# Macaron block of MoE and Mamba on one core: the scan's sum over states by accumulating transfers in SBUF, in two sums, in place of adds on GpSimd

## The chip, the core and the metric

The kernel runs on one core of a Trainium2 chip. A core has five engines with a queue of instructions each: TensorE (PE in the profile, with the weight loads as PEld), VectorE (DVE), ScalarE (ACT), GpSimd (POOL) and SyncE (SP, which here only issues DMAs). They meet through semaphores. SBUF and PSUM are the on-chip memories; transfers are made by 16 DMA engines. The metric is the time of one execution on the device in microseconds (us), the median of a few runs; less is better.

## What is computed

x has 4 sequences of 1024 positions with 128 features. Three sublayers follow each other, each on a layer norm of x: a dense mixture of 8 experts (added at half weight), a Mamba layer, and the same mixture once more. Cut to what matters:

```python
x = x + 0.5 * ffn(layernorm(x))      # sum over 8 experts of cw_e * (silu(x Wg_e) * (x Wu_e)) Wd_e
x = x + mamba(layernorm(x))
x = x + 0.5 * ffn(layernorm(x))

# mamba, 256 channels d, 16 states n
xs, z = split(x @ W_in)
xc = silu(conv4(xs) + conv_b)
dt, B, C = softplus(...), ..., ...   # projections of xc
h[t] = exp(dt[t] * A) * h[t-1] + dt[t] * xc[t] * B[t]     # for each d and n
y[t] = sum over n of h[t] * C[t] + D * xc[t]
out = (y * silu(z)) @ W_out
```

All of it is float32. The sum over n of h C is what the change is about.

## The kernel before, in words

The positions are cut into 8 blocks of 512 (two per sequence); a Mamba block holds its 256 channels as tiles of 128 partitions x 2 x 512, "128x1024" in the profile. There are 16 FFN stages (8 blocks, first and second FFN) in a fixed order (`order`), and TensorE's work on them paces everything: a stage has 16 halves of an expert each taking gate products into PSUM (pg, L543 to L545), up products (pu) and down products (pd, L612, or L598 and L606 where they are split). For each half, ScalarE takes silu of pg (L534) and DVE multiplies it with pu (L559); the next half's pu can't start before that. ScalarE copies pd out (L634); GpSimd (DVE in the first nine experts and in the last stage) weighs it with the broadcast gate weights cwb (L643) and adds it to acc (L646), which TensorE transposes at the end of a stage (L675).

Mamba work is laid between the FFN work by slots. A half has four slots; `run_events` runs at each slot and releases the events of all chains that are due (`START`, `WIDE`, `LATE` and the like give due slots; an event with a condition may wait up to 12 slots longer). A small planner (`Plan`) keeps a model of the time at which each engine will be free. DVE's work is put into two lists, `hi` and `lo`, with a cost and a time from which it is ready; `fill` issues what is due before TensorE's present time. All engines' queues get exactly the order in which Python issues the instructions, so an engine that waits holds back all that is behind it.

A block's states go in pairs (`two`, when `turn` allows it: the list `lo` has at most 9 entries). For each state n:

- ScalarE computes da = exp(dt A) (L861) into a tile of the pool "big" (11 buffers of 128x1024, which also holds dt, dx, cv, zs and the split halves hh, hl and weights wds);
- DVE, `prod` (L875): hb = dx * B into PSUM; B and C of the state are in bcb, which SP broadcasts from DRAM (L696, three buffers, the next one is asked for by `pump` when a product with C is issued);
- DVE, `step` (L887): two scans, one for each 128 channels. At the first it decides `aside` (L882 to L886): if GpSimd's planned backlog is below LOAD = 3.0 us and DVE's list `lo` holds more than LEFT = 6.0 us, the scan writes to da in SBUF and GpSimd makes the product with C; else it stays in PSUM;
- `read`: the last column is kept for the next block (L914 or L900); then da = h * C on DVE (L915), or on GpSimd for a state put aside (L903); then GpSimd adds da to y (L918 or L909). y starts as D * xc (ScalarE, L853).

GpSimd's instructions wait in the list `pend`, first in, first out. `pool_run`, called at each L875, issues from it against a credit of 5.8 us (CAP), and makes each instruction that it issues wait for that L875 (the reason given in the code is "shared SBUF port"). `pool_need` issues all up to a given entry when its result is needed.

When all states of a block are added (`scanned`), `gate` multiplies with silu(z) (GpSimd L944, or DVE L939 in blocks 0 and 7), `outproj` (L955) and `upd` (L962) add the result to x, and the second FFN of that block may begin with its norm statistics (L329 to L341) and gate weights (L418 to L469).

SP's queue holds, in order of issue, the loads of B and C (L696), the broadcasts of the gate weights (L499, L474), the blocks of x (`load_x`, L237; the event at L1048) and the stores of the result.

Of the kernel before, what the change touches and what calls it, by code (L numbers as in the profile page):

```python
# [45 lines left out]
NEVER = 1e9  # L46
WAIT = 12
LOAD = 3.0
LEFT = 6.0
QUEUE = 9  # L50

# [120 lines left out]
def tile_macaron_mamba_moe(  # L172
# [528 lines left out]
    riders, slot, burst_at, want = [], [0], [-1], set()  # L701
    pend, credit = [], [0.0]

    def pool_put(fn, cost, ready, first=False):
        it = [fn, cost, ready, False, None, first]
        pend.insert(sum(o[5] for o in pend) if first else len(pend), it)
        if not plan.lo:
            pool_run(None)
        return it

    def pool_run(after):
        credit[0] = min(credit[0] + CAP, CAP)
        while pend and (after is None or credit[0] > 0.0):
            pool_one(after)

    def pool_one(after):
        it = pend.pop(0)
        credit[0] -= it[1]
        ins = it[0]()
        it[3], it[4] = True, plan.on_pool(it[1], max(it[2], plan.dve))  # L720
        if after is not None:
            tc.add_manual_dep(
                ins.ins, after.ins.name, mybir.DependencyInfo(mybir.DependencyClass.Sync, mybir.DependencyReason.DATA),
                reason="shared SBUF port",
            )

    def pool_need(it):
        if it not in pend:
            plan.need(lambda: it[3])
        while not it[3]:  # L730
            pool_one(None)
        return it[4]


    def mamba_events(k):
# [111 lines left out]

        def dtfin():
            dx = d["dx"] = big(f"dx_{nm}")
            d["dx_it"] = plan.put(lambda: V.tensor_tensor(dx, d["dt"], d["xc"], ALU.mult), 1.14, d["spt"]) if fast else pool_put(lambda: G.tensor_tensor(dx, d["dt"], d["xc"], ALU.mult), 2.4, d["spt"])  # L850
            y = d["y"] = sb.tile([P, ND, TB], F32, tag="y", bufs=2, name=f"y_{nm}")
            d["y_it"] = [
                plan.act_put(lambda i=i: S.activation(y[:, i, :], d["xc"][:, i, :], AF.Copy, scale=D_sb[:, i : i + 1]), 0.61, 0.0)  # L853
                for i in range(ND)
            ]
# [22 lines left out]
        def step(n, i):  # L878
# [10 lines left out]
                0.0 if first else st_sb[:, i, n : n + 1], ALU.mult, ALU.add,  # L889
            )  # L890

        def read(n):
            hb = d.pop("hb")
            da = d.pop(("da", n))
            bcb = d.pop(("bcb", n))
            d.pop(("read", n))
            plan.act_need(*d["y_it"])
            if d["aside"]:
                if not last:
                    V.tensor_reduce(st_sb[:, :, n : n + 1], da[:, :, TB - 1 : TB], AX.X, ALU.max)  # L900

                def weigh():
                    ins = G.tensor_tensor(da, da, bcb[:, 1:2, :].to_broadcast([P, ND, TB]), ALU.mult)  # L903
                    ahead["free"] += 1
                    pump()
                    return ins

                pool_put(weigh, 2.4, plan.dve)
                it = pool_put(lambda: G.tensor_tensor(d["y"], d["y"], da, ALU.add), 2.4, plan.dve)  # L909
                if n == NS - 1:  # L910
                    d["scanned"] = it
                return
            if not last:
                V.tensor_copy(st_sb[:, :, n : n + 1], hb[:, :, TB - 1 : TB])  # L914
            V.tensor_tensor(da, hb, bcb[:, 1:2, :].to_broadcast([P, ND, TB]), ALU.mult)  # L915
            ahead["free"] += 1
            pump()
            it = pool_put(lambda: G.tensor_tensor(d["y"], d["y"], da, ALU.add), 2.4, plan.dve)  # L918
            if n == NS - 1:
                d["scanned"] = it  # L920

        def zproj(i):
                if i == 0:
# [8 lines left out]
        def gate():  # L932
            assert d["zp"] == ND
            d["yg"] = d.pop("zs")
            plan.need(lambda: "scanned" in d)

            if quick:
                def mul():
                    V.tensor_tensor(d["yg"], d["yg"], d["y"], ALU.mult)  # L939

                at = pool_need(d["scanned"])
                d["gated"] = plan.put(mul, 1.14, at)
                return
            d["gated"] = pool_put(lambda: G.tensor_tensor(d["yg"], d["yg"], d["y"], ALU.mult), 2.4, plan.dve)  # L944

        def outproj():
            if quick:
# [82 lines left out]
    def run_events(t):  # L1030
        slot[0] = t
        plan.fill(plan.pe)
        for ch in chains:
            while ch and ch[0][0] <= t:
                at, wait, f = ch[0][:3]
                if len(ch[0]) > 3 and t - at < wait and ch[0][3]() > plan.pe + 0.15:
                    break
                ch.pop(0)
                f()
        chains[:] = [ch for ch in chains if ch]  # L1040

    GPS = E
    add(0, [(0, lambda: load_expert(0))])
    for s in range(len(order)):
        add(8 * GPS * s, ffn_events(s))
        kind, k = order[s]
        if kind == 1 and k + 1 < NBLK:
            add(8 * GPS * s, [(2, lambda k=k: load_x(k + 1))])  # L1048
        add(8 * GPS * (s + 1), [(FENDS.get(s, 16), lambda s=s: ffn_end(s), lambda s=s: max(plan.bank_free(), summed(s)))])
    for k in range(NBLK):  # L1050
        front, mid, back = mamba_events(k)
# [65 lines left out]
```

## Time and profile before

| what | value |
|---|---|
| runs shown, us | 1286.93, 1288.33, 1288.80 (median 1288.33) |
| profiled execution: its own time / its span, us | 1286.3 / 1284.5 |
| ScalarE busy in the span | 70% |
| DMA: bytes moved, mean rate | 113.51 MB, 88 GB/s |
| SP's queue, share of the 16 DMA engines' time | 31.6% |
| GpSimd waiting for DVE's L875 before L918 | 49.0 us in 20 waits |
| starts of FFN stages 4 and 15 (TensorE's first pg) | 327.6 and 1206.3 us |
| updates of x by blocks 0 and 7 (L962) | 278.8 and 1159.1 us |

How to read the lines in the next part: the engine line gives busy time, share of the span and number of instructions. A line by groups has source line, engine, operation, output<-inputs, shapes and number; then busy time and mean nanoseconds of one; then the idle time of the engine just before them and who ended it. A line of waits has the waiting engine and line, whom it waited for, then total us, number of waits, the longest. A line of the chain of waits has start, duration and what was going on; one of the timeline has start, duration, engine, line, operation, and in brackets an idle time before it and its releaser. A line of a stretch gives busy time of PE, PEld, DVE, ACT and POOL, TensorE's granted clock, the share of the DMA engines and the rate.

### The profile page before, as it was taken

The page shows a single profiled execution, that of the slowest core. Times are in us where ns is not written, and L with a number is a line of the kernel's source. Part 1 is how long each engine was busy: PE and PEld are TensorE (multiplying, and loading weights), DVE is VectorE, ACT ScalarE, POOL GpSimd, SP SyncE. Part 2 cuts the span into 40 slices and gives each one's busy share as a digit, 9 for nine tenths or more (in the row PEclk, how much of TensorE's full clock was granted, in tenths as well). Part 3 has the DMA queues.
Part 4 walks back from the last instruction along what each step waited for, and adds up shares of the span by engine and source line. Part 5 has one row for each costly group of instructions (what it writes and reads, how often), then busy time and mean ns, then how long its engine had stood idle before and what let it go on. Part 6 is the DMA issues. An engine that isn't in the chain of part 4 may idle for free.

```text
span 1284.5 us, 14134 instructions
## 1 busy us (share of the span) xinstructions
PE 1255.9 (98%) x4728; PEld 852.4 (66%) x4728; DVE 1102.8 (86%) x1287; ACT 902.0 (70%) x1171; POOL 791.5 (62%) x590
## 2 busy tenths in 40 slices
PE   7999999999999999999999989999999999999998
PEld 5776666666666666666666656666666666668885
DVE  5875589998998999999988979997799999977675
ACT  5775777776778778775867768676877777646663
POOL 1012376767779767786786677787688668663400
PEclk9999999999999999999999999999999999999999
DMA  4420242433232433234333343332234333411110
GB/s 126 139 61 25 77 120 91 107 102 83 82 103 81 126 93 94 86 91 126 94 104 91 71 124 98 101 105 81 67 92 104 110 94 97 114 42 42 34 34 24
DMA packets 72201, 113.51 MB, mean 88 GB/s; under 512 B 7360, under 2 KB 20544, under 8 KB 72128
## 3 DMA queue, kind: packets, MB, share of 16 engines
q1 hardware_dynamic: 72128, 112.61, 31.6%
q8 instruction: 37, 0.61, 0.2%
q14 instruction: 36, 0.29, 0.1%
HBM read 109.71 MB, written 2.88 MB: 88 GB/s over the span
## 4 chain that ended last, share of the span: by engine, by line
PE 77%; DVE 7%; POOL 3%; issue 3%; ACT 3%; DMA 1%; SPq 0%; DVEq 0%; POOLq 0%; ACTq 0%
PE pd L612 23%; PE pu L543 8%; PE pu L544 7%; PE pu L545 7%; PE pg L543 7%; PE pg L545 7%; PE pg L544 7%; PE pd L598 2%; DVE h L559 2%; DVE hb_m L875 2%; DVE hb_m L887 1%; PE pd L606 1%; PE xs_m L767 1%; PE po_m L955 1%; PE dbl_m L813 1%
## 5 line engine op out<-in xcount | busy, mean ns | idle before, releaser
L559 DVE TENSOR_TENSOR h<-h,pu 128x1024 f32<-128x1024 f32 x256 | 311.2, 1216 | 128.8 <-PE pu L545 88.1
L612 PE MATMUL pd<-h,wd 128*128 128x512 f32 x848 | 404.5, 594 | 1.4 <-ACT acc L634 0.7
L534 ACT ACTIVATE h<-pg 128x1024 f32<-128x1024 f32 x256 | 262.8, 1026 | 163.0 <-PE pg L545 156.3
L543 PE MATMUL pg<-xh_f,wh 128*128 128x512 f32 x512 | 272.6, 532 | 1.3 <-ACT xh_f L384 0.7
L918 POOL TENSOR_TENSOR y_m<-y_m,da_m 128x1024 f32<-128x1024 f32 x95 | 229.0, 2410 | 50.0 <-DVE hb_m L875 49.0
L643 POOL TENSOR_TENSOR tmp<-tmp,cwb 128x512 f32<-128x512 f32 x98 | 130.0, 1327 | 182.3 <-ACT tmp L634 77.2
L612 PEld LDWEIGHTS pd<-h,wd 128*128 128x128 f32 x848 | 158.4, 189 | 116.9 <-issue 96.7
L543 PE MATMUL pu<-xh_f,wh 128*128 128x512 f32 x512 | 211.3, 413 | 4.8 <-DVE h L559 4.5
L545 PE MATMUL pg<-xh_f,wl 128*128 128x512 f32 x512 | 202.7, 396 | 0.0
L544 PE MATMUL pg<-xl_f,wh 128*128 128x512 f32 x512 | 202.3, 395 | 0.0
L544 PE MATMUL pu<-xl_f,wh 128*128 128x512 f32 x512 | 202.1, 395 | 0.0
L545 PE MATMUL pu<-xh_f,wl 128*128 128x512 f32 x512 | 202.0, 395 | 0.0
L875 DVE TENSOR_TENSOR hb_m<-dx_m,bcb_m 128x1024 f32<-128x1024 f32 x128 | 181.6, 1418 | 3.0 <-POOL dx_m L850 1.3
L861 ACT ACTIVATE da_m<-dt_m,A_sb 128x512 f32<-128x512 f32 x256 | 163.9, 711 | 0.6
L543 PEld LDWEIGHTS pg<-xh_f,wh 128*128 128x128 f32 x512 | 96.7, 189 | 67.1 <-issue 31.8
L646 POOL TENSOR_TENSOR acc<-acc,tmp 128x512 f32<-128x512 f32 x98 | 130.7, 1333 | 11.5 <-DVE hb_m L875 4.2
L544 PEld LDWEIGHTS pg<-xl_f,wh 128*128 128x128 f32 x512 | 97.1, 190 | 52.5 <-issue 38.9
L887 DVE TENSOR_TENSOR_SCAN hb_m<-da_m,hb_m 128x512 f32<-128x512 f32 x98 | 119.9, 1224 | 2.0
L543 PEld LDWEIGHTS pu<-xh_f,wh 128*128 128x128 f32 x512 | 96.4, 188 | 36.0 <-DVE h L559 11.6
L887 DVE TENSOR_TENSOR_SCAN hb_m<-da_m,st_sb,hb_m 128x512 f32<-128x512 f32 x92 | 118.1, 1284 | 2.1
L915 DVE TENSOR_TENSOR da_m<-hb_m,bcb_m 128x1024 f32<-128x1024 f32 x95 | 115.7, 1218 | 1.3
L544 PEld LDWEIGHTS pu<-xl_f,wh 128*128 128x128 f32 x512 | 96.4, 188 | 24.1 <-issue 3.6
(137 smaller groups left out, 1651.8 us busy)
## 6 DMA issues: line engine op xcount, KB each, us to landing
bcb_m<-bc_m SPq DMA_DIRECT2D x128, 512.0 KB
cwb<-cd_f SPq DMA_DIRECT2D x128, 256.0 KB
x<-in_L_attn_x_dram SPq DMA_DIRECT2D x8, 256.0 KB
wraw<-in_L_ffn_w_gate_dram SPq DMA_DIRECT2D x8, 256.0 KB
wraw<-in_L_ffn_w_up_dram SPq DMA_DIRECT2D x8, 256.0 KB
wd<-in_L_ffn_w_down_dram SPq DMA_DIRECT2D x8, 256.0 KB
out_dram<-x SPq DMA_DIRECT2D x8, 256.0 KB
cd_f<-ct_f SPq DMA_DIRECT2D x64, 4.0 KB
```

The source lines that it names most:

```text
L534: S.activation(h, pg, AF.Silu)
L543: T.matmul(o[:, q, :], wh[e][:, i, cols], d["xh"], start=True, stop=False)
L544: T.matmul(o[:, q, :], wh[e][:, i, cols], d["xl"], start=False, stop=False)
L545: T.matmul(o[:, q, :], wl[e][:, i, cols], d["xh"], start=False, stop=True)
L559: V.tensor_tensor(h, h, pu, ALU.mult)
L612: T.matmul(d["pd"], wd[e][:, cols], h[0], start=(f == 0), stop=(f == FC - 1))
L643: it = put(lambda: G_.tensor_tensor(t, t, cwb, ALU.mult), 1.25, at)
L646: it = put(lambda: G_.tensor_tensor(acc, acc, t, ALU.add), 1.25, at)
L861: S.activation(da[:, i, :], d["dt"][:, i, :], AF.Exp, scale=A_sb[:, i, n : n + 1])
L875: mul = V.tensor_tensor(hb, d["dx"], bcb[:, 0:1, :].to_broadcast([P, ND, TB]), ALU.mult)
L887: V.tensor_tensor_scan((da if d["aside"] else hb)[:, i, :], da[:, i, :], hb[:, i, :], 0.0 if first else st_sb[:, i, n : n + 1], ALU.mult, ...
L918: it = pool_put(lambda: G.tensor_tensor(d["y"], d["y"], da, ALU.add), 2.4, plan.dve)
```

## The change

The adds of da to y on GpSimd (L909 and L918) go. Each is replaced by a DMA that GpSimd issues with accumulate-add: da is added into y in SBUF by the transfer itself (`gather`). There are two sums per block. Even states add into y; state 1's own buffer da becomes the odd sum, into which the other odd states add; after the last state one more transfer adds the odd sum to y (`join`), and that is `scanned` now.

`pend` is no longer first in, first out: each entry belongs to a chain (the even and the odd sum of a block, dx, the FFN's weighted sums), order holds within a chain, and of the chains' heads the one that can start first is issued. A transfer can start when its product is planned to be ready and the transfer before it in its sum has landed, which is planned for 5.9 us after the issue (YDMA); its issue is planned at 0.9 us of GpSimd. Transfers aren't made to wait for an L875 and don't use up the credit. `pool_run` stops at a transfer that could not start within 1.5 us (AHEAD); `pool_flush` in `run_events` issues those that can start.

The rule for putting a state aside is not changed, but the backlog that it looks at has 0.9 us for a transfer where it had 2.4 for an add. `load_x` moves from 2 slots after to 12 slots before the start of a stage, except in the first.

```diff
@@ -46,6 +46,8 @@
 NEVER = 1e9
 WAIT = 12
 LOAD = 3.0
+YDMA = 5.9
+AHEAD = 1.5
 LEFT = 6.0
 QUEUE = 9
 
@@ -701,34 +703,63 @@
     riders, slot, burst_at, want = [], [0], [-1], set()
     pend, credit = [], [0.0]
 
-    def pool_put(fn, cost, ready, first=False):
-        it = [fn, cost, ready, False, None, first]
-        pend.insert(sum(o[5] for o in pend) if first else len(pend), it)
+    def pool_put(fn, cost, ready, chain="w", dma=None):
+        it = [fn, cost, ready, False, None, chain, dma]
+        pend.append(it)
         if not plan.lo:
             pool_run(None)
         return it
 
+    def pool_start(it):
+        at = max(it[2], plan.pool)
+        if it[6] is not None:
+            at = max(at, it[6].get("landed", 0.0))
+        return at
+
+    def pool_next():
+        heads, seen = [], set()
+        for it in pend:
+            if it[5] not in seen:
+                seen.add(it[5])
+                heads.append(it)
+        return min(heads, key=pool_start) if heads else None
+
     def pool_run(after):
         credit[0] = min(credit[0] + CAP, CAP)
         while pend and (after is None or credit[0] > 0.0):
-            pool_one(after)
-
-    def pool_one(after):
-        it = pend.pop(0)
+            it = pool_next()
+            if after is not None and it[6] is not None and pool_start(it) > max(plan.pool, plan.dve) + AHEAD:
+                break
+            pool_one(after, it)
+
+    def pool_one(after, it):
+        pend.remove(it)
+        ins = it[0]()
+        it[3] = True
+        if it[6] is not None:
+            plan.pool = pool_start(it) + it[1]
+            it[4] = it[6]["landed"] = plan.pool - it[1] + YDMA
+            return
         credit[0] -= it[1]
-        ins = it[0]()
-        it[3], it[4] = True, plan.on_pool(it[1], max(it[2], plan.dve))
+        it[4] = plan.on_pool(it[1], max(it[2], plan.dve))
         if after is not None:
             tc.add_manual_dep(
                 ins.ins, after.ins.name, mybir.DependencyInfo(mybir.DependencyClass.Sync, mybir.DependencyReason.DATA),
                 reason="shared SBUF port",
             )
 
+    def pool_flush():
+        while pend:
+            it = pool_next()
+            if it[6] is None or pool_start(it) > max(plan.pool, plan.pe - 1.0):
+                return
+            pool_one(None, it)
+
     def pool_need(it):
         if it not in pend:
             plan.need(lambda: it[3])
         while not it[3]:
-            pool_one(None)
+            pool_one(None, next(o for o in pend if o[5] == it[5]))
         return it[4]
 
 
@@ -847,7 +878,7 @@
 
         def dtfin():
             dx = d["dx"] = big(f"dx_{nm}")
-            d["dx_it"] = plan.put(lambda: V.tensor_tensor(dx, d["dt"], d["xc"], ALU.mult), 1.14, d["spt"]) if fast else pool_put(lambda: G.tensor_tensor(dx, d["dt"], d["xc"], ALU.mult), 2.4, d["spt"])
+            d["dx_it"] = plan.put(lambda: V.tensor_tensor(dx, d["dt"], d["xc"], ALU.mult), 1.14, d["spt"]) if fast else pool_put(lambda: G.tensor_tensor(dx, d["dt"], d["xc"], ALU.mult), 2.4, d["spt"], "x")
             y = d["y"] = sb.tile([P, ND, TB], F32, tag="y", bufs=2, name=f"y_{nm}")
             d["y_it"] = [
                 plan.act_put(lambda i=i: S.activation(y[:, i, :], d["xc"][:, i, :], AF.Copy, scale=D_sb[:, i : i + 1]), 0.61, 0.0)
@@ -889,6 +920,26 @@
                 0.0 if first else st_sb[:, i, n : n + 1], ALU.mult, ALU.add,
             )
 
+        lane = [{}, {}]
+
+        def gather(n, da, at):
+            q = n % 2
+            if n == 1:
+                d["odd"] = da
+            else:
+                to = d["odd"] if q else d["y"]
+                it = pool_put(lambda: G.dma_start(out=to, in_=da, accum_op=ALU.add), 0.9, at, (k, q), lane[q])
+            if n < NS - 1:
+                return
+
+            def join():
+                while any(o[5] == (k, 1) for o in pend):
+                    pool_one(None, next(o for o in pend if o[5] == (k, 1)))
+                return G.dma_start(out=d["y"], in_=d.pop("odd"), accum_op=ALU.add)
+
+            ready = max(at, lane[1].get("landed", 0.0)) + YDMA
+            d["scanned"] = pool_put(join, 0.9, ready, (k, 0), lane[0])
+
         def read(n):
             hb = d.pop("hb")
             da = d.pop(("da", n))
@@ -905,19 +956,15 @@
                     pump()
                     return ins
 
-                pool_put(weigh, 2.4, plan.dve)
-                it = pool_put(lambda: G.tensor_tensor(d["y"], d["y"], da, ALU.add), 2.4, plan.dve)
-                if n == NS - 1:
-                    d["scanned"] = it
+                pool_put(weigh, 2.4, plan.dve, (k, n % 2))
+                gather(n, da, plan.dve + 2.5)
                 return
             if not last:
                 V.tensor_copy(st_sb[:, :, n : n + 1], hb[:, :, TB - 1 : TB])
             V.tensor_tensor(da, hb, bcb[:, 1:2, :].to_broadcast([P, ND, TB]), ALU.mult)
             ahead["free"] += 1
             pump()
-            it = pool_put(lambda: G.tensor_tensor(d["y"], d["y"], da, ALU.add), 2.4, plan.dve)
-            if n == NS - 1:
-                d["scanned"] = it
+            gather(n, da, plan.dve + 0.1)
 
         def zproj(i):
                 if i == 0:
@@ -938,10 +985,10 @@
                 def mul():
                     V.tensor_tensor(d["yg"], d["yg"], d["y"], ALU.mult)
 
-                at = pool_need(d["scanned"])
-                d["gated"] = plan.put(mul, 1.14, at)
+                d["gated"] = plan.put(mul, 1.14, pool_need(d["scanned"]))
                 return
-            d["gated"] = pool_put(lambda: G.tensor_tensor(d["yg"], d["yg"], d["y"], ALU.mult), 2.4, plan.dve)
+            at = pool_need(d["scanned"])
+            d["gated"] = pool_put(lambda: G.tensor_tensor(d["yg"], d["yg"], d["y"], ALU.mult), 2.4, at, (k, 0))
 
         def outproj():
             if quick:
@@ -1030,6 +1077,7 @@
     def run_events(t):
         slot[0] = t
         plan.fill(plan.pe)
+        pool_flush()
         for ch in chains:
             while ch and ch[0][0] <= t:
                 at, wait, f = ch[0][:3]
@@ -1045,7 +1093,7 @@
         add(8 * GPS * s, ffn_events(s))
         kind, k = order[s]
         if kind == 1 and k + 1 < NBLK:
-            add(8 * GPS * s, [(2, lambda k=k: load_x(k + 1))])
+            add(8 * GPS * s, [(2 if s == 0 else -12, lambda k=k: load_x(k + 1))])
         add(8 * GPS * (s + 1), [(FENDS.get(s, 16), lambda s=s: ffn_end(s), lambda s=s: max(plan.bank_free(), summed(s)))])
     for k in range(NBLK):
         front, mid, back = mamba_events(k)
```

## Prediction

> **What bounds the kernel now.** I read the summary of engines first, then the busy time in the stretch where the change acts, then who waits for whom at TensorE, then the costliest groups. From the page:
>
> ```profile
> span 1284.5 us, 14134 instructions
> ...
> PE 1255.9 (98%) x4728; PEld 852.4 (66%) x4728; DVE 1102.8 (86%) x1287; ACT 902.0 (70%) x1171; POOL 791.5 (62%) x590
> ...
> PEclk9999999999999999999999999999999999999999
> ```
>
> TensorE is busy for 98% of the span at an undisturbed clock, and the diff changes no matmul. The time can fall only by what TensorE loses in waits. The state work (first product of states to last block's end) lies between about 100 and 1160 us; busy time there:
>
> ```profile
> core 0: us, PE busy (x) PEld busy (x) DVE busy (x) ACT busy (x) POOL busy (x), PEclk, DMA share, GB/s
> 100.00:1160.00 1060.00, 1049.00 (x3856) 691.89 (x3855) 945.39 (x1077) 761.38 (x992) 758.29 (x539) 1.00 0.34 93
> ```
>
> TensorE idles 1060.0 - 1049.0 = 11.0 us of this stretch, DVE is busy 89%, GpSimd 72%, the DMA engines 34%. "Idle" misses some waits: matmuls are pipelined (0.39 us long, started 0.23 us apart), so I also went through the start times of all matmuls in the trace and added up what each gap has beyond the usual gap between the same pair of lines: 41 us in all, some 24 of them between 100 and 1160 us. That 24 us (1.9%) is all that any relief of DVE or GpSimd can win. Who ends the waits of the weight loads, from the list of waits at TensorE:
>
> ```profile
> PEld pg L543 <- ACT h L534: 14.9, 31, 1.3
> PEld pu L543 <- DVE h L559: 11.6, 19, 1.9
> ...
> PEld v_m L834 <- DVE dbs_m L822: 5.9, 4, 3.7
> ...
> PEld cwt_f L467 <- POOL cw_f L458: 2.7, 5, 0.8
> ```
>
> (A weight load may wait 0.2 us at no cost, so these are more than matmuls lose: in the count by gaps, ScalarE's h is 6.5 us, DVE's h 6.2, DVE's dbs 4.9, GpSimd together some 2.) The largest single stall is one of dbs, and it isn't DVE's load that makes it. In the chain of waits and the timeline of DVE and TensorE:
>
> ```profile
> 732.94 3.35 POOL da_m L903
> ...
> 736.71 5.55 DMA x<-in_L_attn_x_dram
> 742.26 0.02 issue
> ```
>
> ```profile
> 742.28 0.87 DVE L329 BATCH_NORM_STATS2 st_f<-x 128x6 f32<-128x128 f32 x4 [3.44 <-DMA x<-in_L_attn_x_dram]
> ```
>
> ```profile
> 745.38 0.51 PE L834 MATMUL v_m<-dbs_m,wdt_h 128*128 128x512 f32 x1 [3.24 <-DVE dbs_m L822]
> ```
>
> SP's load of x stood behind two loads of B and C (L696) which waited for a buffer that GpSimd's C product (L903) held; the load landed 5.55 us after its issue, DVE's statistics stood still for 3.44 us with dbs queued behind them, and TensorE lost 3.4 us there and 0.9 us just after: 4.3 us.
>
> **The change, part by part.** The groups that it touches:
>
> ```profile
> L918 POOL TENSOR_TENSOR y_m<-y_m,da_m 128x1024 f32<-128x1024 f32 x95 | 229.0, 2410 | 50.0 <-DVE hb_m L875 49.0
> ...
> L875 DVE TENSOR_TENSOR hb_m<-dx_m,bcb_m 128x1024 f32<-128x1024 f32 x128 | 181.6, 1418 | 3.0 <-POOL dx_m L850 1.3
> ...
> L915 DVE TENSOR_TENSOR da_m<-hb_m,bcb_m 128x1024 f32<-128x1024 f32 x95 | 115.7, 1218 | 1.3
> ```
>
> ```profile
> L909 POOL TENSOR_TENSOR y_m<-y_m,da_m 128x1024 f32<-128x1024 f32 x33 | 83.4, 2527 | 2.5
> L903 POOL TENSOR_TENSOR da_m<-da_m,bcb_m 128x1024 f32<-128x1024 f32 x33 | 81.0, 2453 | 18.7 <-DVE hb_m L875 18.7
> ```
>
> 1. *Removed:* 95 + 33 = 128 adds on GpSimd, 229.0 + 83.4 = 312 us of its 791.
>
> 2. *Added:* per block 15 transfers (state 1 gives its own buffer to the odd sum) and one join, 8 x 16 = 128 transfers of 128x1024 f32, 512 KB each, issued by GpSimd. No such operation is in this trace. GpSimd's time for one issue: at least the 0.36 us that SP takes for a B and C load of the same size; at most a whole add, 2.4 us. I take the planner's 0.9, between the two and nearer to SP's row: 128 x 0.9 = 115 us, so GpSimd is relieved by about 200 us (bounds +5 and +266). Landing: the nearest row is the B and C load, 4.79 us on the chain of waits at 254.59 us; an add must also read its destination, so at most twice that, 9.6. I take 5.9, the planner's, nearer to the row. The Trainium skill, in "DMA: Bandwidth & Descriptors", section "Anatomy of one DMA", gives 2.0 us plus the bytes at 436 GB/s for a DMA issued by GpSimd, an estimate of 3.2 us; no run here shows it, and with 3.2 in place of 5.9 the forecast would not move.
>
> What waits for a landing: the next add of the same sum. 128 states take from 148 to 1136 us (first and last L875), 7.7 us each, so with two sums the next add comes 15.4 us later on average and some 10 us in a burst: 5.9 is covered, 9.6 just. Behind a transfer that does wait stand GpSimd's other instructions: norm statistics (L338 to L341), gate weights (L446 to L458), weighted sums (L643, L646).
>
> DMA engines: a B and C load is 256 packets of about 0.118 us on 16 engines, 1.9 us of them all; an add takes between that and twice that, so 128 of them 243 to 486 us, 23 to 46 points on 34%. B and C loads then land up to some 4 us later, hidden by three buffers: one is asked for when the product with C is done and needed two states, 15 us, later.
>
> One rule speaks against issuing from GpSimd. The copies that DVE makes of SBUF data are L914's, 49 in the whole trace, 7.7 us in all, 157 ns each. By "SBUF — State Buffer" of the Trainium skill, section "SBUF: two separate sides", GpSimd can't write descriptors while DVE runs such a copy in a two-port mode. No run here shows this; by it 7.7 us of GpSimd's time at most would be lost off TensorE's path, against none.
>
> 3. *More C products on GpSimd.* A state goes aside (L882 to L886) when GpSimd's backlog is under 3 us and DVE's list is over 6 us. Per state of 7.7 us GpSimd now has 2.4 (add) + 2.1 (weighted sums) + 0.6 (33 of 128 C products) + 0.4 = 5.5 us. With 0.9 for the add, the same load is reached when 0.87 of the states are aside; 0.26 are now. The list of over 6 us will often be missing when DVE is relieved; I take the middle, 0.55, that is 70 states: DVE loses 37 x 1.22 = 45 us (bounds 0 and 78 x 1.22 = 95), from 945 to 900 of 1060, 85%. DVE's L875 has a median of 1.23 us and a mean of 1.42: 128 x 0.19 = 24 us spent behind GpSimd's instructions; with 128 fewer adds and 37 more products perhaps a third goes, 8 us. All of this lies beside TensorE. What it is worth is a part of DVE's waits in the stretch: h 6.2 and the remaining dbs, xl and others some 4, together 10. With DVE down by 5 to 6% of its load I take a third: -3 us (bounds: 0 and -10; that the new order makes TensorE wait more is rival (b)).
>
> 4. *load_x* moves 14 slots (some 16 us) ahead of its place in SP's queue, for all stages but the first. x has six buffers and the old contents are stored a stage before, so it waits for none. It goes ahead of the B and C load that held it at 732 us: -4.3 us (bounds 0, if another SP wait takes its place, and -4.3). What is late next there is the wait for the buffers themselves, which DVE isn't behind.
>
> 5. *The end of a block.* The last add lands (5.9), the join lands (5.9), against one add of 2.4: the sum is ready some 10 us later. Cover: block 0's x is updated at 278.8 us and its second FFN starts at 327.6; block 7's at 1159.1, with the FFN at 1206.3. The preparations take some 16 to 20 us of these 47 to 49; without this cover it would be 10 us each, 20 in all.
>
> 6. *Buffers:* counted from the trace, at most 8 of the 11 "big" buffers hold live data. The odd sum keeps one for a whole block, and a second one where blocks meet: 10. ScalarE's exponentials would wait at 12.
>
> Sum, against the profiled execution (span 1284.5, its own time 1286.3): -4.3 - 3 = -7.3, about 1 us given back for transfers that GpSimd waits for: -6, so 1280. The median of the runs shown, 1288.33, is 2 above that execution, so **1282**, 0.5% below.
>
> **The rivals.** (a) *Only x counts*: DVE's load isn't what makes the short stalls (their releasers are the order of instructions, with 6.5 us on ScalarE), or few more states go aside: 1288.3 - 4.3 = 1284, down to no gain at all if x's stall reappears, 1288. For it: DVE's h waits are 19 waits of 0.6 us, scattered. (b) *Slower, waits at the head of GpSimd's queue*: a landing of over 10 us, the pace of a burst, makes the transfer hold back what TensorE needs: 16 gate weights, 16 sums, 24 norm statistics, 56 places. At 0.3 us lost at each, 17 us, less 4.3: +13, 1301; it decides from landings over 10 us, or from an issue that costs GpSimd as much as an add. For it: the DMA engines go to 57 to 80%, and no accumulating transfer has a row here. Against it: the 15.4 us mean spacing. (c) *Much faster*: all 10 us of DVE's waits, GpSimd's 2 and x go: 1288.3 - 16 = 1272. Against it: ScalarE's waits stay, and the fixed order is only a plan.
>
> **How the numbers follow.** Forecast (1277 to 1285): 0.48. (c): 0.07. (a): 0.14, half of it faster by over 0.2%, half within; 0.2% (2.6 us) is about what a measurement of this kernel can tell from no change. (b): 0.31, of which 0.02 within 0.2%. Faster 0.48 + 0.07 + 0.07 = 0.62; same 0.07 + 0.02 = 0.09; slower 0.29. The range reaches from 1274, inside (c), to (b)'s 1301; beyond lie 0.06 and 0.12. The forecast and (a) alone give 1277 to 1288.
>
> **What would show it.** GpSimd's adds gone and its busy time near 791 - 312 + 37 x 2.45 = 570; C products on DVE down from 95 to near 58; no idle time at L834 near 742; TensorE idle under 8 us in the stretch. Wrong: GpSimd's small instructions waiting for landings, TensorE waiting longer at L467, L675 or L359, ScalarE's exponentials waiting for buffers, or the same sum of short waits with DVE's load lower.

## The result, and the profile after

The changed kernel takes 1294.23 us (median; 1291.84 to 1294.94) where the kernel before, on the same chip, takes 1287.97 (1286.11 to 1288.8): a ratio of 1.0049, with a 95% interval of 1.0034 to 1.0064. It is 6 us slower; the forecast was 6 us faster. The profiled execution takes 1294.15 us with a span of 1292.4, 7.9 above the span before.

The page of the changed kernel, as before: span, engines, DMA queues (packets, MB, share of 16 engines), groups, and DMA issues with their median time from issue to landing:

```profile
span 1292.4 us, 14294 instructions
...
PE 1257.2 (97%) x4728; PEld 853.9 (66%) x4728; DVE 1050.8 (81%) x1253; ACT 901.5 (70%) x1171; POOL 660.3 (51%) x624
...
q1 hardware_dynamic: 72128, 112.61, 31.8%
q0 software_dynamic: 18432, 67.12, 26.5%
...
L954 POOL TENSOR_TENSOR da_m<-da_m,bcb_m 128x1024 f32<-128x1024 f32 x67 | 161.5, 2411 | 47.0 <-DVE hb_m L906 47.0
L906 DVE TENSOR_TENSOR hb_m<-dx_m,bcb_m 128x1024 f32<-128x1024 f32 x128 | 169.9, 1327 | 11.1 <-DMA bcb_m<-bc_m 8.1
...
y_m<-da_m POOLq DMA_DIRECT2D x72, 512.0 KB, 9.1
...
da_m<-da_m POOLq DMA_DIRECT2D x56, 512.0 KB, 9.5
```

The relief came as planned: DVE is down by 52 us, GpSimd by 131 (the 660 include 117 us of DMA issues), 67 states are aside (before 33). TensorE does the same matmuls in a longer span. The transfers land 9.1 and 9.5 us after their issue, not 5.9. A new name stands in front of DVE's L906: it now waits for the loads of B and C. Busy time in the stretch where the change acts (PE, PEld, DVE, ACT, POOL, granted clock, DMA share, GB/s):

```profile
100.00:1160.00 1060.00, 1041.86 (x3815) 686.32 (x3814) 887.60 (x1037) 757.45 (x989) 625.95 (x572) 1.00 0.67 156
```

TensorE idles 18.1 us here, where it idled 11.0: 7.1 of the 7.9 us are in this stretch. DVE is busy 84% (was 89%), and the DMA engines 67% (was 34%). The list of waits (waiting engine and line, whom it waited for: total us, times, longest) names what is new:

```profile
POOL y_m L938 <- DMA da_m<-da_m: 68.2, 8, 11.2
...
POOL acc L645 <- DMA cwb<-cd_f: 24.2, 4, 11.7
...
DVE hb_m L906 <- DMA bcb_m<-bc_m: 8.1, 10, 1.7
...
DVE zs_m L986 <- DMA y_m<-da_m: 7.2, 1, 7.2
```

L938 is the join at a block's end: GpSimd stands still 8.5 us on average, eight times, until the odd sum's last transfer has landed. L645 (weighted sums) waits for gate weights that come late. L906 and L986 are DVE's. The one stall of x at 742 us, which the prediction saw, is gone: in my count of matmul start gaps, the bin 700 to 750 us falls from 5.5 to 0.6 us. In its place are many: 250 to 300 rises from 2.1 to 6.8, 750 to 800 from 0 to 4.5, 200 to 250 from 1.1 to 2.8. All gaps together rise from 40.9 to 48.8 us, by the 7.9 that the span grew.

The largest of them is block 0's end. The timelines of GpSimd, DVE and TensorE there (start, duration, engine, line, what; in brackets the idle time before it and who ended it):

```profile
262.94 0.87 POOL L931 DMA_DIRECT2D da_m<-da_m  x1
271.92 0.86 POOL L938 DMA_DIRECT2D y_m<-da_m  x1 [8.11 <-DMA da_m<-da_m]
```

```profile
276.49 1.23 DVE L986 TENSOR_TENSOR zs_m<-zs_m,y_m 128x1024 f32<-128x1024 f32 x1 [7.24 <-DMA y_m<-da_m]
277.63 0.68 DVE L681 TENSOR_TENSOR x<-x,fo 128x512 f32<-128x512 f32 x1
```

```profile
278.37 1.86 PE L1002 MATMUL po_m<-w_out_sb,zs_m 128*128 128x128 f32 x7 [4.94 <-DVE x L681]
```

The odd sum's last transfer is issued at 262.94 and lands 9 us later; the join is issued at 271.92 and lands 4.5 us later; DVE's gate multiply (L986) stands at the head of its queue for 7.24 us, and L681 behind it. TensorE's output projection L1002, which reads L986's zs and comes after L681, stands at the head of TensorE's queue for 4.94 us. The next reader of block 0's x, the norm statistics of its second FFN (L331), starts at 311.6 us, 28 us after the update; the loss is in what stands in line.

The stall costs more than its length. The stretch just behind it, in the columns of the stretch above:

```profile
278.40:281.70 3.30, 3.30 (x15) 3.30 (x16) 3.23 (x3) 0.00 (x0) 0.00 (x0) 0.50 0.76 188
```

The granted clock is 0.50 here, for 3.41 us by the clock's records, and the 16 products of L1002 start 213 ns apart; those of the other seven blocks, at a clock of 1.00, 112 ns. That is 1.7 us more for the 16. The kernel before has such a stretch too, which the tenths of its page hide: 3.41 us at 0.50 from 746.8 us, just behind the stall of x, for 1.8 us.

A B and C load that lands late does the same in small. DVE and TensorE 95 us later:

```profile
367.46 1.60 DVE L906 TENSOR_TENSOR hb_m<-dx_m,bcb_m 128x1024 f32<-128x1024 f32 x1 [1.69 <-DMA bcb_m<-bc_m]
```

```profile
372.14 0.50 PE L400 MATMUL lt_f<-xh_f,wrg_h 128*128 128x512 f32 x1 [1.63 <-DVE xl_f L389]
```

DVE loses 1.69 us, then runs without a gap until L389, 4 us later, for which TensorE waits 1.63 us.

Before SP can issue a load, a product with C must give a buffer back. SP's own waits for these products, before and after:

```profile
SPq L696 <- DVE da_m L915: 426.8, 76, 18.3
SPq L696 <- POOL da_m L903: 177.5, 27, 16.5
```

```profile
SPq L698 <- POOL da_m L954: 351.8, 49, 13.7
SPq L698 <- DVE da_m L964: 203.2, 35, 27.7
```

Twice as many states are aside, so the waits behind GpSimd double and those behind DVE halve. The sum of the two doesn't grow (604 and 555 us) and isn't itself the lateness. A state aside gives its buffer back after GpSimd's product and not DVE's; the load is then issued together with the transfer that the same product made ready, into DMA engines that are 67% busy. From each load's issue to the last count on its semaphore, and to the start of the L906 (before, L875) that uses it:

| kernel | landing, median and slowest tenth, us | issue to use, median and shortest tenth, us | waits of DVE |
|---|---|---|---|
| before | 5.0, 6.0 | 14.1, 9.4 | none |
| changed | 6.3, 9.9 | 12.5, 6.5 | 10 |
| e4 below: 29 states aside | 5.9, 8.3 | 13.8, 10.1 | none |
| e5 below: adds kept, same traffic | 5.9, 8.0 | 14.2, 9.1 | none |

The loads land later in all three kernels with transfers, but only in the changed one, with 67 states aside, is a tenth of them issued less than 6.5 us before its use; DVE waits where both meet. The gate weights land after 5.4 us (median) and 10.8 (slowest tenth), before 3.8 and 6.3.

### The profile page after: what moved, and what is told of

Its sections match the earlier page's. It is cut to its first block, busy times and chain, and to the rows that moved or that the text cites. A ratio compares the mean times of both kernels' runs of the same rounds, so it can differ in the third digit from the quotient of the medians.

```text
span 1292.4 us, 14294 instructions
## 1 busy us (share of the span) xinstructions
PE 1257.2 (97%) x4728; PEld 853.9 (66%) x4728; DVE 1050.8 (81%) x1253; ACT 901.5 (70%) x1171; POOL 660.3 (51%) x624
## 3 DMA queue, kind: packets, MB, share of 16 engines
q0 software_dynamic: 18432, 67.12, 26.5%
## 4 chain that ended last, share of the span: by engine, by line
PE 73%; DMA 6%; DVE 4%; ACT 4%; issue 3%; POOL 3%; SPq 0%; POOLq 0%; DVEq 0%; ACTq 0%
PE pd L614 21%; PE pu L545 7%; PE pg L545 7%; PE pu L547 7%; PE pu L546 7%; PE pg L547 7%; PE pg L546 7%; DMA bcb_m<-bc_m 3%; PE pd L600 2%; DMA da_m<-da_m 2%; PE pd L608 1%; DMA y_m<-da_m 1%; DVE h L561 1%; PE xs_m L798 1%; ACT da_m L892 1%
## 5 line engine op out<-in xcount | busy, mean ns | idle before, releaser
L561 DVE TENSOR_TENSOR h<-h,pu 128x1024 f32<-128x1024 f32 x256 | 311.1, 1215 | 176.0 <-PE pu L547 124.4
L645 POOL TENSOR_TENSOR tmp<-tmp,cwb 128x512 f32<-128x512 f32 x98 | 137.1, 1399 | 208.6 <-ACT tmp L636 76.6
L954 POOL TENSOR_TENSOR da_m<-da_m,bcb_m 128x1024 f32<-128x1024 f32 x67 | 161.5, 2411 | 47.0 <-DVE hb_m L906 47.0
L906 DVE TENSOR_TENSOR hb_m<-dx_m,bcb_m 128x1024 f32<-128x1024 f32 x128 | 169.9, 1327 | 11.1 <-DMA bcb_m<-bc_m 8.1
L648 POOL TENSOR_TENSOR acc<-acc,tmp 128x512 f32<-128x512 f32 x98 | 137.1, 1399 | 7.7
L547 PEld LDWEIGHTS pu<-xh_f,wl 128*128 128x128 f32 x512 | 96.7, 189 | 22.6
L547 PEld LDWEIGHTS pg<-xh_f,wl 128*128 128x128 f32 x512 | 96.5, 189 | 22.6
L636 ACT COPY tmp<-pd 128x512 f32<-128x512 f32 x111 | 64.7, 583 | 66.6 <-PE pd L614 55.1
```

Source lines behind the costliest of these rows:

```text
L547: T.matmul(o[:, q, :], wl[e][:, i, cols], d["xh"], start=False, stop=True)
L561: V.tensor_tensor(h, h, pu, ALU.mult)
L636: S.copy(t, pd)
L645: it = put(lambda: G_.tensor_tensor(t, t, cwb, ALU.mult), 1.25, at)
L648: it = put(lambda: G_.tensor_tensor(acc, acc, t, ALU.add), 1.25, at)
L906: mul = V.tensor_tensor(hb, d["dx"], bcb[:, 0:1, :].to_broadcast([P, ND, TB]), ALU.mult)
```

## The experiments

**Theory.** The earlier x gains what was forecast. The rest loses: transfers that land after 9 us, B and C buffers that GpSimd's products hold, and loads that these two make late leave DVE and GpSimd waiting at the heads of their queues; DVE's relief earns nothing. **Rivals:** the DMA traffic by itself slows the loads or the engines; the planner's wrong landing time (5.9 for 9.4) spoils the order; the order is merely an unlucky one. Ratios are to the kernel before, with the 95% interval; 0.001 is 1.3 us.

**e1: only the earlier x**, in the kernel before:

```diff
-            add(8 * GPS * s, [(2, lambda k=k: load_x(k + 1))])
+            add(8 * GPS * s, [(2 if s == 0 else -12, lambda k=k: load_x(k + 1))])
```

> The kernel before with nothing of the change but the earlier load of x. All theories: the 3.4 us stall at L834 near 742 us and the 0.9 us after it go, ratio to before 0.9967 (-4.3 us), if what the prediction says of this step holds. Rival: another wait of SP or DVE takes its place, ratio 1.000.

Measured: 0.9957 (0.9945 to 0.9970), 1281.20 us, the fastest of all with e14. Everything else in the change, put on top of this step, therefore costs 0.0092, 11.8 us. Its trace has no stretch at half the clock between 100 and 1160 us.

**e11: all but the earlier x**, the changed kernel with that line put back.

> The changed kernel with the load of x at its old place. The first experiment says that the earlier load is worth 5 us by itself: ratio 1.008 to 1.010 if the parts add up. If the load finds SP's queue free in the changed kernel anyway: 1.005, and the earlier load bought nothing here.

Measured: 1.0151 (1.0126 to 1.0175). The step is worth 13 us here and 5.5 in the kernel before, so effects don't simply add. One reason is the clock: this trace has 17.1 us at a granted clock of 0.50 between 100 and 1160 us, in four stretches, where the changed kernel has 3.4. The chain of waits shows the old stall made worse:

```profile
172.78 0.36 SPq L698
173.14 0.05 issue
173.19 9.35 DMA x<-in_L_attn_x_dram
```

A load of x again goes out right behind a B and C load (L698) and now lands after 9.35 us, where 5.55 were shown before; DVE's norm statistics wait 14.8 us for x in three waits.

**e14: DVE loaded more.** e1 with no state put aside:

```diff
-                d["aside"] = load < LOAD and left > LEFT
+                d["aside"] = False
```

> The first experiment's kernel (adds on GpSimd, earlier x, 33 states aside, 0.9957) with no state put aside: DVE makes all 128 products with C, 40 us more. This tells what DVE's load is worth to TensorE. The prediction's step (a third of DVE's 10 us of waits for 45 us of load) would give +3 us: ratio 0.998. If DVE's load is hidden at this level: 0.9957 within 0.001. GpSimd is 80 us less busy, which can only help.

Measured: 0.9955 (0.9943 to 0.9967). The stretch in e1 and in e14:

```profile
100.00:1160.00 1060.00, 1052.20 (x3877) 694.46 (x3876) 952.86 (x1088) 763.65 (x995) 756.85 (x540) 1.00 0.35 93
```

```profile
100.00:1160.00 1060.00, 1053.99 (x3878) 695.24 (x3877) 977.90 (x1121) 758.85 (x992) 666.41 (x507) 1.00 0.35 93
```

DVE has 25 us more to do and TensorE idles 6.0 us, not 7.8. GpSimd has 90 us less to do in the same run, so DVE's load isn't varied alone; but 25 us more of it, with that relief beside it, cost TensorE nothing. That the 58 us which the change took off DVE had no taker fits this; no run takes load off DVE and changes nothing else.

**e9: the traffic alone.** e1, with a plain copy of 512 KB in SBUF issued by SP after each B and C load (BIG = 9 for the room):

```diff
             nc.sync.dma_start(out=t, in_=stored[k]["bc"][:, n, :].partition_broadcast(P))
+            nc.sync.dma_start(out=side[n % 2], in_=wh[0].bitcast(F32))
```

> The first experiment's kernel (0.9957) with a plain copy of 512 KB within SBUF, issued by SP after each load of B and C into buffers that nothing reads; GpSimd, TensorE, ScalarE and DVE have the same instructions in the same order. Traffic alone, without GpSimd's time, without accumulation and without anything that waits for it but SP. Theory B alone (loads come late by traffic): ratio 1.000 or more. Theory E (traffic counts only where something stands ready for it, that is with more products on GpSimd or with landings that are waited for): within 0.002 of 0.9957.

Measured: 0.9962 (0.9950 to 0.9975), not told apart from e1, with the stretch:

```profile
100.00:1160.00 1060.00, 1052.14 (x3876) 694.54 (x3876) 952.91 (x1088) 763.90 (x996) 757.65 (x540) 1.00 0.50 157
```

The bytes per second are those of the changed kernel (157 and 156 GB/s), the DMA engines are at 50%, B and C loads land after 7.1 us in the slowest tenth (e1: 6.2), and TensorE loses nothing. Bytes alone aren't the cause. (The engines' share stops at 0.50, since a plain copy takes less of them than an accumulating one; 0.67 by itself was not tried without GpSimd's part.)

**e5: adds and accumulating traffic.** e1, with an accumulating transfer of 512 KB issued by GpSimd after each add, into a buffer that nobody reads:

```diff
+        G.dma_start(out=side[n % 2], in_=wh[0].bitcast(F32), accum_op=ALU.add)
```

> The first experiment's kernel (adds on GpSimd, x loaded earlier, 0.9957), with each add followed by an accumulating transfer of 512 KB into a buffer that nothing reads; the order on TensorE, ScalarE and DVE is the same, and 9 big buffers stand in for 11 to make room. So it has the change's traffic and nothing waits for a landing except the next transfer into the same buffer. Theory B (traffic): loads of B and C land as late as in the changed kernel (90th percentile 7 us or more) and the ratio to before rises to 1.000 or more. Against B: ratio within 0.002 of 0.9957. GpSimd also has 128 x 0.9 us more to issue, which can add some.

Measured: 1.0133 (1.0117 to 1.0148). It doesn't separate what it was to separate: each issue takes 0.895 us of GpSimd, which is 115 us more on an engine that kept its adds, and DVE's product is held up more often:

```profile
L884 DVE TENSOR_TENSOR hb_m<-dx_m,bcb_m 128x1024 f32<-128x1024 f32 x128 | 206.7, 1615 | 3.8 <-POOL dx_m L859 2.2
```

In e1 the same product has a mean of 1448 ns. TensorE waits for h 14.7 us in 17 waits (e1: 4.5 in 8). So 22 us lie between e5 and e9 of the same number of bytes, and GpSimd's time, the accumulation and the longer products share them in a way that this run can't divide. Two things it does show. With the changed kernel's DMA share (0.67) and rate (155 GB/s) DVE never waits for B and C, as the table above has it. And an issue by itself doesn't hold DVE's product up: the products that meet nothing but issues on GpSimd take 1.22 to 1.23 us, 10 of them here and 17 in the changed kernel; all the excess falls on those that meet GpSimd's other instructions.

**e6: half the bytes per transfer.** The changed kernel with `out=to[:, 0, :], in_=da[:, 0, :]` in `gather`; the second 128 channels are left out of the sums, except in the join.

> The changed kernel with transfers of half the size (the adds of the second 128 channels are left out, but in the join), the same instructions in the same order otherwise. Theory B: landing falls from 9.4 to some 7 us, the DMA engines' share from 67% to some 53%, and half or more of the loss comes back: ratio 1.001 or less. Theory D (more C products on GpSimd) without traffic: ratio stays near 1.005.

Measured: 0.9986 (0.9977 to 0.9995). **e7: half the bytes per B and C load.** Only B is loaded; the products with C use B.

> The changed kernel with only B loaded and used in C's place too (the product with C is left out, B's stands for it), so each load has 256 KB in place of 512, with the same instructions in the same order. Theory B: transfers start earlier (landing from 9.4 to some 7 us) and loads land earlier, ratio 1.001 or less. If what costs is the time from the release of a buffer to its use, not the DMA engines' load, it also falls. Only if neither counts: 1.005.

Measured: 0.9984 (0.9975 to 0.9993). Each brings 8 us. In e6 transfers land after 7.6 us, DVE waits 3.0 us for B and C and 5.8 at L986; in e7 after 7.0, DVE waits 0.6 and 4.6. So in this kernel, unlike in e9, the load on the DMA engines does cost. (Half a transfer and half a load are also sooner done; the two runs don't tell a freer engine from a shorter transfer.)

**e4: fewer states aside.** The changed kernel with `and n % 4 == 1` in the condition: 29 states.

> The changed kernel with states put aside only where n mod 4 is 1: 29 C products on GpSimd in place of 67 (33 before), all sums by transfers. Theory D (the additional C products on GpSimd hold the buffers of B and C longer, and so the loads come late): ratio to before falls to 1.001 or less. Theories A and B: these products aren't what costs, ratio 1.004 or more, with DVE some 40 us busier than in the changed kernel.

Measured: 0.9984 (0.9975 to 0.9993), 8 us better. **e12** is e4 with e6's half transfers (the second 128 channels left out as there).

> 29 C products on GpSimd, as in the fourth experiment (0.9984), and transfers of half the size, as in the sixth (0.9986; adds of the second 128 channels left out). If traffic and the products on GpSimd each cost for themselves, both come back: 0.992. If they cost only together, one of the two removed is enough: 0.997 to 0.999.

Measured: 0.9964 (0.9952 to 0.9977), the level of e1. With as few states aside as before, the full-size transfers cost little (0.9984 against e1's 0.9957); with half the bytes as well, nothing that can be told from none. e4's stretch:

```profile
100.00:1160.00 1060.00, 1050.14 (x3861) 693.26 (x3860) 934.64 (x1083) 766.54 (x997) 529.50 (x535) 1.00 0.67 157
```

The DMA share is the 0.67 of the changed kernel, DVE has 47 us more to do and TensorE idles 9.9 us where it idled 18.1; DVE no longer waits for B and C at all. So the larger part of the loss needs the traffic and the asides together: 8 us return when either is halved, and not 16 but 11 when both are. (67 states aside without any transfer were not run.)

**e10: a fourth buffer for B and C** in the changed kernel (`bufs=4`, `"free": 4`, BIG = 10 for the room); only SP's order differs.

> The changed kernel with four buffers for B and C in place of three (and ten big buffers in place of eleven); only SP's order differs. If DVE's 8.1 us of waits for B and C, and what they cost TensorE, are a main part of the loss: DVE waits under 2 us for these loads, ratio 1.001 or less. If not, ratio 1.004 or more.

Measured: 1.0020 (1.0010 to 1.0031), 4 us better. Of DVE's new waits for loads and transfers one is left:

```profile
DVE zs_m L986 <- DMA y_m<-da_m: 5.1, 1, 5.1
```

**e3: block 0's sum as adds on GpSimd**, all else as in the changed kernel, so that this block's end waits for no landing (`fast` holds for block 0 alone; 112 transfers are left, and 61 states are aside):

```diff
+            if fast:
+                it = pool_put(lambda: G.tensor_tensor(d["y"], d["y"], da, ALU.add), 2.4, at, (k, 0))
+                if n == NS - 1:
+                    d["scanned"] = it
+                return
...
-                pool_put(weigh, 2.4, plan.dve, (k, n % 2))
+                pool_put(weigh, 2.4, plan.dve, (k, 0 if fast else n % 2))
```

> The changed kernel, but block 0 sums by GpSimd's adds as before; the other seven blocks by transfers. Theory A: block 0 has the one place where a landing stands in DVE's queue with TensorE behind it, so some 6 us come back: ratio to before 1.000. Theory B: one block in eight less traffic, so an eighth of the loss comes back: ratio 1.004 to 1.005.

Measured: 1.0026 (1.0015 to 1.0037), 3 us better. L986's wait and the stretch at half the clock behind it are gone, which were 6.6 us of TensorE in the changed kernel; about half of that is lost again elsewhere. **e13** joins e10 and e3.

> The changed kernel with both repairs: four buffers for B and C (alone 1.002) and block 0 summed by adds (alone 1.0026); the change is at 1.005 and the earlier load of x alone at 0.9957. If late loads and block 0's awaited landings are two separate parts of the loss, both come back: ratio 0.999 to 1.000, and what is left to 0.9957 is the other block ends and scatter. If they overlap: 1.002.

Measured: 0.9997 (0.9988 to 1.0005). The two repairs add up (1.0049 - 0.0029 - 0.0023 = 0.9997), which speaks against the rival of an unlucky order without excluding it, and 5 us to e1 are left; 1.4 of them lie, in its trace, in one stretch of 3.41 us at half the clock, at 660.6 us. GpSimd still waits 47.6 us for joins and 37.7 for gate weights in e13; which of it TensorE pays for wasn't settled.

**e8: the join as an add on GpSimd** in place of the last transfer, planned for both sums' landing:

```diff
-                return G.dma_start(out=d["y"], in_=d.pop("odd"), accum_op=ALU.add)
+                return G.tensor_tensor(d["y"], d["y"], d.pop("odd"), ALU.add)
```

> The changed kernel with the join done as an add on GpSimd (2.4 us) in place of a transfer, the other 120 transfers unchanged. Theory A, in the form that is left (waiting for two landings one after the other at a block's end): block 0's stall of 5.1 us shrinks by some 2 to 3 us, and so does the time at the other block ends where they count: ratio 1.002 to 1.003. Otherwise 1.005.

Measured: 1.0135 (1.0114 to 1.0156), a miss. Block 0's end, GpSimd and DVE:

```profile
270.87 2.34 POOL L938 TENSOR_TENSOR y_m<-y_m,da_m 128x1024 f32<-128x1024 f32 x1 [7.84 <-DMA da_m<-da_m]
```

```profile
273.25 2.28 DVE L987 TENSOR_TENSOR zs_m<-zs_m,y_m 128x1024 f32<-128x1024 f32 x1 [7.21 <-POOL y_m L938]
275.45 1.21 DVE L561 TENSOR_TENSOR h<-h,pu 128x1024 f32<-128x1024 f32 x1
```

The sum is ready 3 us earlier than in the changed kernel, and DVE's wait is as long (7.21 us), but the plan, which believes in an earlier landing, has put the gate multiply ahead of an FFN product h (L561), and TensorE loses 6.5 us there alone, and more to a clock of 0.50 behind it. The landing costs by what stands behind the instruction that waits.

**e2, e15, e16: the planner's landing time** in the changed kernel (`YDMA = 5.9` becomes 9.4, 7.0 and 5.0).

> The changed kernel with the planner told that a transfer lands 9.4 us after its issue (the median in its trace), not 5.9. Theory A (the loss is the planner's wrong landing time: engines wait at the heads of their queues for landings that were planned earlier): TensorE's 5.1 us at block 0's output product goes, GpSimd's 68 us before the joins fall under 20, ratio to before at or under 1.000. Theory B (the loss is the traffic itself: transfers and loads of B, C and gate weights delay each other on the DMA engines): the ratio stays within 0.002 of the change's 1.005. Theory C (orders laid out differently just scatter by some us): anything from 0.998 to 1.006, with stalls at new places.

> The changed kernel with the planner's landing time at 7.0 us (5.9 in the change, 9.4 gave 1.0128). Theory C (each order has its own scatter, and the planner's number matters little by itself): anything from 1.002 to 1.013, not between the two in any orderly way. If the plan's landing time matters in one direction: 1.005 to 1.009.

> The changed kernel with the planner's landing time at 5.0 us. As for the 7.0: theory C allows 1.002 to 1.013; if a longer planned landing is what costs (1.0128 at 9.4), 5.0 gives 1.005 or less.

| planned landing, us | states aside | ratio (95% interval) |
|---|---|---|
| 5.0 (e16) | 65 | 1.0044 (1.0032 to 1.0057) |
| 5.9 (as changed) | 67 | 1.0049 (1.0034 to 1.0064) |
| 7.0 (e15) | 66 | 1.0071 (1.0056 to 1.0086) |
| 9.4 (e2) | 63 | 1.0128 (1.0114 to 1.0142) |

The nearer the plan comes to the measured landing, the slower the kernel, though the first two rows can't be told apart. A wrong landing time in the plan is not the cause, and the row climbs in order, which doesn't look like chance. In e2 block 0's wait at L986 is gone, as it should be with a true landing time, but the joins still hold GpSimd 54.9 us, and two other waits have grown:

```profile
POOL acc L645 <- DMA cwb<-cd_f: 44.2, 7, 16.9
...
DVE hb_m L906 <- DMA bcb_m<-bc_m: 12.5, 12, 3.9
```

With 5.9 they were 24.2 and 8.1. One of these waits for B and C, 3.87 us at L906, ends at 1023.8 us; TensorE then waits 4.05 us for h, and 3.41 us at a clock of 0.50 follow. Why the loads come later with this plan stays open.

## Why the prediction was wrong

- *What bounds the kernel* held: 7.1 of the 7.9 us of span came as TensorE's idle time in the stretch. The clock was not quite "undisturbed": both kernels have one stretch of 3.41 us at 0.50, each behind a long stall.
- *Steps 1 and 2, GpSimd's time:* right. The 128 adds went, an issue takes 0.88 us (median; 0.9 taken), the engines give 26.5% of 1292.4 us to 128 transfers, 2.7 us each (1.9 to 3.8), and the DMA share is 0.67 (0.57 to 0.80).
- *Step 2, the landing:* **the first step that failed.** 5.9 us was taken, between 4.79 and 9.6; the median is 9.4, at the far bound. The source view of L931 has the least, the median and the most:

```profile
DMA to landing us min/median/max: 4.4/9.4/13.3
```

  A lone transfer lands even sooner than was taken (4.4; the joins, which mostly run alone, 4.5). What failed was to price it alone. Its first packet starts 1.4 to 9.0 us after the issue. Where at most one of SP's loads of B and C or gate weights is in flight or issued within 1 us (25 transfers), it starts after 1.5 us and the transfer lands after 5.3 (medians); where two or more are (103 transfers), after 4.8 and 9.9. The C product that makes the transfer ready also frees the buffer for the next B and C load, so this is the usual case. The Trainium skill, "DMA: Bandwidth & Descriptors", section "Issuing engines are not separate DMA queues", says that transfers of all issuers run on the same 16 engines and interleave. The sharing agrees with these starts; a first packet that waits some 3 us longer beside two loads isn't stated there.
- *Step 2, the rule against issuing from GpSimd:* the lines were misread. L914 copies the last column of hb, which lies in PSUM, so these 49 are not copies of SBUF data, and this kernel can't test the rule with them. The issues took 0.85 to 1.24 us.
- *Step 2, "hidden by three buffers":* **failed too.** It was reckoned with the time between states, 15 us, and not with a buffer that GpSimd's product holds. A tenth of the loads had under 6.5 us from issue to use (before 9.4), DVE waited 8.1 us for B and C, and a fourth buffer gives back 4 us (e10).
- *Step 3, more C products on GpSimd:* the number was right (67 for 70; DVE 888 us in the stretch for 900), and L906's time over its usual 1.23 us fell by 12 us (8 forecast). The worth was wrong: -3 us were taken, and nothing in the runs shows a gain from DVE's relief (e14 loads DVE by 25 us at no cost). Worse, the products moved aside are a condition of the loss: with 29 aside 8 of the 11.8 us come back (e4). By "SBUF — State Buffer" of the Trainium skill, section "SBUF: two separate sides", a DVE instruction with two inputs in SBUF and a GpSimd instruction that reads SBUF exclude each other on a shared port for the whole of an instruction. The excess of this product agrees: 24.1 us before, 12.5 after, 27.9 in e1 and 49.3 in e5, all of it in products that meet GpSimd's other instructions and none in those that meet only issues.
- *Step 4, x:* right, -4.3 forecast, -5.5 measured alone (3.9 to 7.1 by the interval). The stall's second part was taken at 0.9 us; by the matmuls' starts the half clock behind it cost 1.8.
- *Step 5, a block's end:* **failed.** The cover is real for x (28 us to its next reader), but the wait stands at the head of DVE's and TensorE's queues, in the middle of FFN work: 4.94 us of TensorE at block 0 and 1.7 at half the clock behind it, and 3 us back with adds in that block (e3). Block 7's gate multiply, DVE's too, doesn't wait for a landing.
- *Step 6, buffers:* right; ScalarE's exponentials wait 0.6 us in all.
- *The sum:* x -5.5, the rest +11.8, where -4.3 and -2 were forecast. Rival (b) named the side, and its condition was a landing of over 10 us or a costly issue. The loss came with a landing just below that, and was 12 us, not the 17 it was given. The parts that are known lie elsewhere than rival (b) had them: 4 us at DVE's queue, through SP's late loads (e10), and 3 us at block 0's end (e3). The last 5 us stay open, and GpSimd's waits may have a part in them.

## What to carry to other kernels

Relief of an engine that doesn't bound is worth the waits it ends and no more; load that engine on purpose first (as e14 did) and see whether anyone notices. Price an added transfer by its landing beside the loads that the same event sets off, and price the wait for it by what stands behind the waiting instruction in each queue, not by when its result is needed. Look at the granted clock just behind a long stall of TensorE; between 100 and 1160 us each of the 15 stalls of over 2.5 us in these traces came with 3.4 us or more at half the clock. Where a change has a small part beside the large one, run the small part alone: here one line held all the gain.

## What the runs showed of the hardware

An accumulating transfer of 512 KB within SBUF lands 4.4 us after its issue at best and 9.4 in the median beside B and C loads; a 4 KB packet of it takes some 0.33 us, one of e9's plain copies 0.16. A plain copy of the same size beside each load took the DMA engines to 50% and cost TensorE nothing (e9). GpSimd itself is held 0.9 us for each transfer that it issues. DVE's product takes its usual 1.22 to 1.23 us beside such an issue (27 cases in e5 and the changed kernel); in e5, with 128 issues on a GpSimd that kept its adds, its mean went from 1448 to 1615 ns, all of it beside GpSimd's other instructions. Behind the stall of 4.94 us at block 0's end TensorE's granted clock was 0.50 for 3.41 us, and matmuls started 213 ns apart where 112 were usual.
